# Layer 1's x with tokens on partitions, by 32x32 squares on VectorE and transfers through DRAM in place of TensorE transposes

## The chip, the cores and the metric

The kernel runs on one core of a Trainium2 chip. The core has TensorE (PE, matrix products), VectorE (DVE), ScalarE (ACT), GpSimd (POOL) and SyncE (SP), which issues the transfers, and 16 DMA engines. Each engine runs its own instructions in the order in which they were written into its queue, and waits on semaphores for the others. The metric is the device time of one execution in microseconds (us). Before the change it is 2448.67 us, the median of 3 runs (2447.55 to 2448.9).

## The reference

Four layers work one after the other on x of shape (4, 512, 32, 32), in fp32: 4 batches, 512 channels, 1,024 tokens. Layer 0 is an attention with 8 heads, layer 1 a linear attention, layer 2 an attention with one head and a layer norm ahead of it, layer 3 an attention with 4 heads and a group norm. The change lies in layer 1:

```python
Q = jnp.einsum('bcn,mc->bmn', xf, wq) + bq[None, :, None]
K = jnp.einsum('bcn,mc->bmn', xf, wk) + bk[None, :, None]
V = jnp.einsum('bcn,oc->bon', xf, wv) + bv[None, :, None]
gate = (jnp.max(xf, axis=-1) + jnp.mean(xf, axis=-1))[:, :, None]
V = gate * V
Qf = jax.nn.softplus(Q).transpose(0, 2, 1)
Kf = jax.nn.softplus(K)
KV = jnp.einsum('bmn,bcn->bmc', Kf, V)
norm = 1.0 / jnp.einsum('bnm,bm->bn', Qf, jnp.sum(Kf, axis=-1) + EPS)
wval = jnp.einsum('bnm,bmc,bn->bcn', Qf, KV, norm)
return x + gamma * wval
```

M is 64: queries and keys have 64 features for each of the 1,024 tokens.

## The kernel before

A batch's x lies in SBUF as `[128, 4, 1024]`: 128 channels of a chunk on the partitions, 4 chunks, 1,024 tokens. Every product of two fp32 matrices is two TensorE instructions of up to 512 columns; a transpose is one.

Layer 1 doesn't compute V. The kernel multiplies the keys with x first and with wv after: `keys_times_x` sums K's features times x over the tokens (64 x 512), `transpose_kx` turns that, and `keys_times_values` multiplies it with `wv1`. A product that sums over tokens needs both operands with tokens on the partitions. For x that is `transpose_x(i)`, i = 0 to 3: two blocks of 128 tokens, 4 chunks each, so 8 TensorE transposes into one two-bank PSUM tile (L1438), and a copy of 128x1024 to SBUF, by ScalarE for even i (L1445) and VectorE for odd i (L1443). For the keys it is `transpose_keys` (L1453). The SBUF places for x come from `scratch`, four tiles which `softplus` (e, u, l) and `gates` use as well; xt of i goes to `scratch((i + 3) % 4)`. In batches 0 to 2 they are the tiles `v` of the next batch's layer 0, in batch 3 they are from the pool `pt`.

Layer 1 has no stage of its own. `linear_attention` returns a list of 16 small functions ("pieces"), and the projections of another piece of work call `slot()` after every few products, which takes one piece off the list. For batches 0 to 2 that is `project_qkv` of the next batch in layer 0: one slot after the first 16 products, then a slot after every two calls of `seven_products` (L712), and the last pieces in `project_v` (L837). For batch 3 the pieces stand between products of layer 2's weights (L646) and its first projection. The pieces are, in order: gates, features of both token halves (the second ends with softplus), x's transposes 0, 1, 2, the keys' transposes, x's transposes 3, `keys_times_x` 0 and 1, `keys_times_x` 2 and 3 with `sum_keys`, `divide_queries`, `transpose_kx`, `keys_times_values`, an empty one, and two updates of x.

TensorE keeps the order in which its instructions are written (`manual_schedule`). The other engines' order is set by a planner, which goes by the order of the code as a priority and fills an engine's gaps with what is ready. SP's transfers stand in one queue. DRAM tiles are used already: x of a finished batch is stored to `home` and read back, and the quotients of the attention take a way through `quotients` to be spread over partitions.

softplus (L1390 to L1396) goes back and forth between VectorE and ScalarE and ends with a VectorE instruction that writes `feat`, the queries' and keys' features (`block` in the profile).

Of the kernel before, what the change touches and what calls it, by code (L numbers as in the profile page):

```python
# [13 lines left out]
F32 = mybir.dt.float32  # L14
# [4 lines left out]
P = 128  # L19
# [3 lines left out]
NC = C // P  # L23
NT = S // P
TB = 512
NTB = S // TB
QT = TB // P
M = 64
GROUP = 16
LIMIT = 1e18  # L30


# [18 lines left out]
def general_path(ctx: ExitStack, tc: tile.TileContext, d: dict, out: bass.AP):  # L51
# [41 lines left out]
    for b in range(1, B):  # L93
# [19 lines left out]

    gmat = const.tile([P, P // GROUP, GROUP], F32, name="gmat")
    nc.vector.memset(gmat, 1.0 / GROUP)
    nc.gpsimd.affine_select(
        out=gmat, in_=gmat, pattern=[[-GROUP, P // GROUP], [0, GROUP]],
        compare_op=ALU.is_ge, fill=0.0, base=0, channel_multiplier=1,
    )
    nc.gpsimd.affine_select(  # L120
        out=gmat, in_=gmat, pattern=[[GROUP, P // GROUP], [0, GROUP]],
        compare_op=ALU.is_ge, fill=0.0, base=GROUP - 1, channel_multiplier=-1,
    )
# [351 lines left out]
def plain_path(ctx: ExitStack, tc: tile.TileContext, d: dict, out: bass.AP, count):  # L475
# [11 lines left out]
    nc = tc.nc  # L487
# [7 lines left out]
    dram = ctx.enter_context(tc.tile_pool(name="dram", bufs=1, space=bass.MemoryType.DRAM))  # L495
# [3 lines left out]
    def acc_tile():  # L499
        return ps_acc.tile([P, TB], F32, tag="acc", name="acc")  # L500

    def two_tile(name):
        return ps_sc.tile([P, 2, TB], F32, tag="sc", name=name)

    def row_tile(name):
        return work.tile([P, TB], F32, tag="row", bufs=3, name=name)
# [7 lines left out]
    def many_tile(name):  # L514
        return work.tile([P, NC, TB], F32, tag="many", name=name)
# [9 lines left out]
    def chunks_tile(tag, name, bufs=1):  # L525
        return work.tile([P, NC, TB], F32, tag=tag, bufs=bufs, name=name)
# [69 lines left out]


    wv1 = chunks_tile("xn", "wv1", 2)
    nc.sync.dma_start(wv1, d["wv1"].rearrange("(c p) o -> p c o", p=P))
    block1 = chunks_tile("xn", "block1", 2)  # L600
    wqk1 = block1[:, 0, :].rearrange("p (c o) -> p c o", c=NC)
    nc.sync.dma_start(wqk1, d["wqk1"].rearrange("(c p) o -> p c o", p=P))
# [15 lines left out]
    ident = const.tile([P, P], F32, name="ident")  # L618
# [9 lines left out]

    gmat = const.tile([P, P // GROUP, GROUP], F32, name="gmat")
    nc.vector.memset(gmat, 1.0 / GROUP)  # L630
# [36 lines left out]
    idle = lambda: None  # L667
# [3 lines left out]
    def both(*fs):  # L671
        return lambda: [f() for f in fs]
# [194 lines left out]
    def project_qkv(wqkv, bias, src, vt, room, first=False, between=lambda: None):  # L867

        q = q_tiles()
        k = work.tile([P, NC, S], F32, tag="k", name="k")  # L870
        inputs = lambda j, tb: src(tb)[:, 2 * j : 2 * j + 2, :]
        made = []

        def sums():
            with tc.issue_after(closing.pop()) if closing else nullcontext():
                made.extend(sum_inputs([pt_tile("t") for _ in range(4)], inputs))
            return made


        seven_products(  # L880
            NC,
            lambda i, j, o: wqkv[:, 2 * j : 2 * j + 2, i * C + o * P : i * C + (o + 1) * P],
            inputs,
            lambda i, o: col(bias, i * NC + o),
            lambda i, tb, o: k[:, o, bass.ts(tb, TB)] if i else q[tb][:, o, :],
            sums,
            slots=1,
            first=first,
        )

        assert len(pieces) <= 7
        wv = wqkv[:, :, 2 * C :]
        between()
        project_v(vt, wv, inputs, made, room())
        return q, k
# [502 lines left out]
    def linear_attention(b, scratch):  # L1398

        x = xs[b]  # L1400
        t = {}
        flat = lambda tile: tile.rearrange("p a s -> p (a s)")
# [29 lines left out]
            nc.vector.tensor_scalar(gate, gate, gamma, None, ALU.mult)  # L1432

        def transpose_x(i):
            ps = two_tile("xt")
            for s in range(2):
                for c in range(NC):
                    nc.tensor.transpose(  # L1438
                        ps[:, s, bass.ts(c, P)], x[:, c, bass.ts(2 * i + s, P)], ident
                    )  # L1440
            t["xt", i] = scratch((i + 3) % 4)
            if i % 2:
                nc.vector.tensor_copy(t["xt", i], ps)  # L1443
            else:
                nc.scalar.copy(t["xt", i], ps)  # L1445

        def transpose_keys():

# [16 lines left out]
        def keys_times_x(i):  # L1465
            if i == 0:
                t["kx"] = acc_tile()
            xt = t.pop(("xt", i))

            for s in range(2):  # L1470
                nc.tensor.matmul(  # L1471
                    t["kx"][s * M : (s + 1) * M, :], lhsT=t["kf"][:, 2 * i + s, :],
                    rhs=xt[:, s, :], start=(i == 0), stop=(i == NT // 2 - 1),
                )
            if i == NT // 2 - 1:
                kx = row_tile("kx")
                nc.scalar.copy(kx, t["kx"])
                t["kx"] = kx
# [47 lines left out]
        def update(a):  # L1526
# [15 lines left out]
            lambda: features(0),  # L1542
            lambda: features(1),
            lambda: transpose_x(0),
            lambda: transpose_x(1),
            lambda: transpose_x(2),
            transpose_keys,
            lambda: transpose_x(3),
            both(lambda: keys_times_x(0), lambda: keys_times_x(1)),
            both(lambda: keys_times_x(2), lambda: keys_times_x(3), sum_keys),  # L1550
            divide_queries,
            transpose_kx,
# [102 lines left out]
    def verdict():  # L1655

        assert next(unit) <= UNITS
        ok = const.tile([P, 2 * UNITS], F32, name="ok")
        nc.vector.tensor_scalar(ok, tops.rearrange("p a n -> p (a n)"), LIMIT, None, ALU.is_le)
        row = const.tile([P, 1], F32, name="row")  # L1660
# [6 lines left out]
    with tc.manual_schedule(engines={mybir.EngineType.PE}):  # L1667
# [8 lines left out]
        for b in range(B):  # L1676
            vt = v_tiles()
            if b > 0:
                pieces.extend(linear_attention(b - 1, lambda i: vt[i]))
            q, k = project_qkv(  # L1680
                wqkv0, "bqkv0", lambda tb: xs[b][:, :, bass.ts(tb, TB)], vt,
                lambda: chunks_tile("ot", "ws"), first=(b == 0),
                between=outputs_bias,
            )
            flush()
            if b > 0:
                away(b - 1)
                if b + 1 < B:
                    nc.sync.dma_start(x_tile(b + 1), xin[b + 1])
                else:  # L1690
                    back(0)
            if b == 0:
                os = output_sums(wo0)
            if b == B - 1:
                w2 = wpool.tile([P, 3 * NC, C], F32, tag="wqkv", name="w2")
                nc.sync.dma_start(w2, d["w2"].rearrange("(c p) o -> p c o", p=P))
            attention(
                b, q, lambda c, j: k[:, c, bass.ts(j, P)], vt, 8, 64.0**-0.5, wo0, os, bo0[0],
                plain=(b == B - 1),
            )  # L1700
# [31 lines left out]
        flush()  # L1732
        wo2 = load_wo(d["wo2"])
        lin = linear_attention(B - 1, lambda i: pt_tile("l1"))

        norms[1][0]()
# [4 lines left out]
        for o in range(NC):  # L1741
            ps = gps.get(o)
            if ps is None:
                ps = acc_tile()
# [5 lines left out]
        for o in range(NC):  # L1750
            ps = acc_tile()
# [85 lines left out]
        for b in range(B):  # L1837
            vt = v_tiles()

            q, k = project_qkv(  # L1840
                wqkv3, "bqkv3", lambda tb: ready[tb], vt,
                lambda: wpool.tile([P, NC, C], F32, tag="wo", name="ws") if b == 0
                else chunks_tile("ot", "ws"),
            )
# [20 lines left out]
@with_exitstack  # L1865
def conv_seq(ctx: ExitStack, tc: tile.TileContext, d: dict, out: bass.AP):
    nc = tc.nc
    flag = ctx.enter_context(tc.tile_pool(name="flag", bufs=1))
    count = flag.tile([1, 1], mybir.dt.int32, name="count")
    plain_path(tc, d, out, count)  # L1870
    good = nc.values_load(count, min_val=0, max_val=P)
    with tc.If(good < P):
        general_path(tc, d, out)
# [56 lines left out]
```

## Time and profile before

| what | value |
|---|---|
| median of 3 runs | 2448.67 us |
| the profiled execution | 2449.81 us |
| its span from first to last instruction | 2448.0 us |
| PE busy | 2430.2 us (99%) |
| VectorE busy | 1490.6 us (61%) |
| ScalarE busy | 705.6 us (29%) |
| transposes of x (L1438) | 128, listed at 272 ns each |
| copies of xt by ScalarE (L1445), by VectorE (L1443) | 8 at 1.01 us, 8 at 1.22 us |
| products of keys and x (L1471) | 64, 592 ns each |
| moved by DMA | 87.59 MB, 36 GB/s on average |

Busy time is the union of an engine's instructions. TensorE's instructions overlap, so the distance between two starts, not the listed duration, is what one of them takes from the engine. A line number is that of the instruction in the code below; a group `xt<-ident,x` writes the tile xt and reads ident and x. An entry in square brackets at the end of a timeline row is the engine's idle time before it and who ended it.

### The profile page before, as it was taken

What the parts mean: (1) busy time and instruction counts of PE and PEld (TensorE: products, weight loads), DVE (VectorE), ACT (ScalarE), POOL (GpSimd) and SP (SyncE); (2) the same over time, 40 slices, a digit from 0 to 9 for tenths busy, and PEclk for the clock granted to TensorE, in tenths of its full rate; (3) what the DMA queues carried; (4) which work ended last, traced back from release to release, by engine and by line L of the source; (5) the groups of instructions that cost most, each with busy time, mean ns of one, the idle gap of its engine ahead of it and who ended that gap; (6) DMA issues with size and microseconds to landing.
All of it is one profiled execution on the core that took longest, in us unless ns stands there. A gap on an engine that the chain in (4) does not pass through costs nothing.

```text
span 2448.0 us, 24708 instructions
## 1 busy us (share of the span) xinstructions
PE 2430.2 (99%) x10130; PEld 1220.0 (50%) x10130; DVE 1490.6 (61%) x1778; ACT 705.6 (29%) x868; POOL 248.3 (10%) x240
## 2 busy tenths in 40 slices
PE   9999999999999999999999999999999999999998
PEld 4544544453455344644645446445556456555653
DVE  3577577757765788556595775764554554445344
ACT  1454144415531653221211201112321430321132
POOL 4001100110010002101103021021020001002000
PEclk9999999999999999999999999999999999999999
DMA  5000020002001211011001020110010001000001
GB/s 185 6 13 18 1 78 10 18 1 79 19 9 38 102 27 43 1 69 52 17 0 69 5 85 1 52 69 17 35 69 0 18 35 52 0 35 35 0 27 40
DMA packets 28799, 87.59 MB, mean 36 GB/s; under 512 B 2604, under 2 KB 10284, under 8 KB 25735
## 3 DMA queue, kind: packets, MB, share of 16 engines
q1 hardware_dynamic: 28678, 85.95, 9.7%
q8 instruction: 81, 1.33, 0.2%
q14 instruction: 40, 0.32, 0.0%
HBM read 60.59 MB, written 25.35 MB: 35 GB/s over the span
## 4 chain that ended last, share of the span: by engine, by line
PE 98%; DVE 1%; DMA 0%; ACT 0%; issue 0%; SPq 0%; DVEq 0%
PE acc L712 20%; PE acc L837 12%; PE acc L987 9%; PE sc L941 9%; PE acc L972 9%; PE sc L936 9%; PE acc L844 8%; PE acc L1089 7%; PE acc L1321 6%; PE acc L1282 2%; PE acc L1023 1%; PE acc L646 1%; PE upd L1531 1%; PE acc L1471 1%; PE feat L1413 1%; PE xt L1438 1%
## 5 line engine op out<-in xcount | busy, mean ns | idle before, releaser
L946 ACT ACTIVATE pt<-sc 128x1024 f32<-128x1024 f32 x384 | 379.2, 1022 | 541.2 <-PE sc L941 304.0
L955 DVE TENSOR_TENSOR sum<-sum,pt 128x1024 f32<-128x1024 f32 x256 | 314.5, 1228 | 160.4 <-ACT pt L946 147.4
L972 PE MATMUL acc<-pt,v 64*64 64x512 f32 x2048 | 246.7, 591 | 0.0
L936 PE MATMUL sc<-q,k 64*64 64x512 f32 x2048 | 244.3, 591 | 1.1 <-ACT pt L946 1.1
L987 PE MATMUL acc<-pt,v 128*128 128x512 f32 x512 | 240.8, 594 | 0.0
L941 PE MATMUL sc<-q,k 128*128 128x512 f32 x512 | 239.8, 593 | 0.0
L712 PE MATMUL acc<-t,ws 128*128 128x512 f32 x384 | 173.9, 593 | 0.0
L700 POOL TENSOR_TENSOR ws<-wqkv 128x256 f32<-128x256 f32 (+1 forms) x40 | 37.0, 926 | 1309.9 <-PE acc L1023 519.5
L952 DVE TENSOR_TENSOR sum<-pt 128x1024 f32<-128x1024 f32 x64 | 78.0, 1219 | 137.4 <-ACT pt L946 137.4
L987 PEld LDWEIGHTS acc<-pt,v 128*128 128x128 f32 x512 | 96.6, 190 | 125.3 <-issue 121.6
L941 PEld LDWEIGHTS sc<-q,k 128*128 128x128 f32 x512 | 96.8, 190 | 116.1 <-issue 92.9
L972 PEld LDWEIGHTS acc<-pt,v 64*64 64x64 f32 x2048 | 78.6, 133 | 142.2 <-issue 137.8
L936 PEld LDWEIGHTS sc<-q,k 64*64 64x64 f32 x2048 | 77.4, 133 | 140.8 <-issue 130.7
L712 PEld LDWEIGHTS acc<-t,ws 128*128 128x128 f32 x384 | 72.5, 190 | 86.6 <-issue 85.4
L751 ACT COPY v<-acc 128x512 f32<-128x512 f32 x24 | 14.0, 585 | 306.2 <-PE acc L837 287.9
L683 DVE RECIPROCAL rd<-acc 128x512 f32<-128x512 f32 (+1 forms) x24 | 80.5, 3353 | 29.1 <-PE acc L1023 29.1
L837 PE MATMUL acc<-ws,t 128*128 128x256 f32 x384 | 86.8, 379 | 0.0
L844 PE MATMUL acc<-qs,w 128*128 128x512 f32 x192 | 86.3, 592 | 0.0
L844 PE MATMUL acc<-q,ln 128*128 128x512 f32 x192 | 85.8, 593 | 0.0
L1089 PE MATMUL acc<-ot,wo 128*128 128x256 f32 x336 | 80.6, 383 | 3.2 <-ACT ou L1108 2.7
L742 DVE TENSOR_TENSOR v<-acc,v 128x512 f32<-128x512 f32 x72 | 49.6, 689 | 53.7 <-PE acc L837 53.7
L751 ACT COPY q<-acc 128x512 f32<-128x512 f32 x40 | 23.4, 585 | 197.5 <-PE acc L712 197.5
(328 smaller groups left out, 3450.1 us busy)
## 6 DMA issues: line engine op xcount, KB each, us to landing
home<-x SPq DMA_DIRECT2D x8, 2048.0 KB
x<-home SPq DMA_DIRECT2D x8, 2048.0 KB
out<-x SPq DMA_DIRECT2D x32, 256.0 KB
rds<-quotients SPq DMA_DIRECT2D x30, 256.0 KB
rds<-quotients SPq DMA_DIRECT2D x7, 1024.0 KB
x<-in_x SPq DMA_DIRECT2D x3, 2048.0 KB
wo<-in_wo SPq DMA_DIRECT2D x3, 1024.0 KB
w<-in_w SPq DMA_DIRECT2D x1, 3072.0 KB
```

The source lines that it names most:

```text
L683: nc.vector.reciprocal(rd, ps)
L712: nc.tensor.matmul(ps, lhsT=w[:, m, :], rhs=x[:, m, :], start=start, stop=stop, skip_group_check=True)
L837: nc.tensor.matmul(ps[:, bass.ts(r, C // 2)], lhsT=x[:, m, bass.ts(2 * o + r, P)], rhs=w[:, m, :], start=(start and r == 0), stop=stop, sk ...
L844: nc.tensor.matmul(ps, lhsT=x[:, m, bass.ts(o, P)], rhs=w[:, m, :], start=start, stop=stop, skip_group_check=True,)
L936: nc.tensor.matmul(ps[half(h), s, :], lhsT=key(g, i)[half(s), half(h)], rhs=q[qb][half(s), g, :], start=True, stop=True,)
L941: nc.tensor.matmul(ps[:, s, :], lhsT=key(g, 2 * i + s), rhs=q[qb][:, g, :], start=True, stop=True)
L946: exps.append(nc.scalar.activation(pt, ps, AF.Exp, scale=scale).ins)
L955: adds.append(nc.vector.tensor_tensor(acc, acc, pt, ALU.add).ins)
L972: nc.tensor.matmul(outs[qb, g][r][half(s), :], lhsT=v[i // 2][half(r), i % 2, g * P + s * hd : g * P + (s + 1) * hd], rhs=pt[half(r), s, : ...
L987: nc.tensor.matmul(outs[qb, g][0], lhsT=v[j // 2][:, j % 2, bass.ts(g, P)], rhs=pt[:, s, :], start=(j == 0), stop=(j == NT - 1),)
L1089: nc.tensor.matmul(ps[i][:, bass.ts(o, n)], lhsT=w[:, m, bass.ts(o, P)], rhs=t[:, m, :], start=(start and m + o == 0), stop=(stop and m == ...
L1321: nc.tensor.matmul(ps[i, o], lhsT=w[m][:, bass.ts(o, P)], rhs=t[m], start=(start and m == 0), stop=(stop and m == 3), skip_group_check=True,)
```

## The change

`transpose_x(i)` is written anew and called twice for each batch, each call for 512 tokens. Two VectorE instructions of 128x1024 elements transpose squares of 32x32: within each group of 32 partitions, 32 channels and 32 tokens change places. The result, `squares`, has tokens on the partitions, but only 32 of them, and a quarter of the channels in each group of partitions. Four transfers, one for each group of 32 partitions, store it to a DRAM tile `home` in rows of 2 KB (1 MB in all). Two transfers of 512 KB read it back in rows of 1 KB, with 128 tokens on the partitions, into the same four `scratch` places as before. `squares` is the tile of the tag `many`, of which there is one; of `home` there are two.

The channels of xt then stand in another order: group of 32, chunk, channel within the 32. `keys_times_x` picks one token block's columns out of xt as runs of 32 elements with a step of 64, and `wv1` is loaded with its rows in that order, by four transfers of 32 partitions in place of one.

In the list of pieces, x's transposes are pieces 4 and 5; the places of the former third and fourth are empty. The keys' transposes stand in the same, seventh place, between the two empty ones.

```diff
-    nc.sync.dma_start(wv1, d["wv1"].rearrange("(c p) o -> p c o", p=P))
+
+    rows = d["wv1"].rearrange("(c a j) o -> c j a o", c=NC, a=NC)
+    for c in range(NC):
+        nc.sync.dma_start(wv1[c * SQUARE : (c + 1) * SQUARE], rows[c])
...
         def transpose_x(i):
-            ps = two_tile("xt")
-            for s in range(2):
-                for c in range(NC):
-                    nc.tensor.transpose(
-                        ps[:, s, bass.ts(c, P)], x[:, c, bass.ts(2 * i + s, P)], ident
-                    )
-            t["xt", i] = scratch((i + 3) % 4)
-            if i % 2:
-                nc.vector.tensor_copy(t["xt", i], ps)
-            else:
-                nc.scalar.copy(t["xt", i], ps)
...
+            squares = many_tile("squares").rearrange(
+                "p r (h n j) -> p r h n j", h=2, n=2 * NC
+            )
+            for h in range(2):
+                k = 2 * i + h
+                nc.vector.transpose(
+                    squares[:, :, h].rearrange("p r n j -> p n r j"),
+                    x[:, :, k * 2 * P : (k + 1) * 2 * P].rearrange(
+                        "p c (n j) -> p c n j", j=SQUARE
+                    ),
+                )
+            home = dram.tile([NC, NC, SQUARE, TB], F32, tag="squares", bufs=2, name="squares")
+            for a in range(NC):
+                nc.sync.dma_start(
+                    home[a].rearrange("r i f -> i r f"),
+                    squares[a * SQUARE : (a + 1) * SQUARE].rearrange("p r h n j -> p r (h n j)"),
+                )
+            for h in range(2):
+                xt = t["xt", 2 * i + h] = scratch((2 * i + h + 3) % 4)
+                nc.sync.dma_start(
+                    flat(xt).rearrange("p (a f) -> p a f", a=NC),
+                    home.rearrange("a r i (h f) -> h (r i) a f", h=2)[h],
+                )
...
-            xt = t.pop(("xt", i))
+            xt = flat(t.pop(("xt", i))).rearrange("p (b s j) -> p s b j", s=2, j=SQUARE)
...
-                    rhs=xt[:, s, :], start=(i == 0), stop=(i == NT // 2 - 1),
+                    rhs=xt[:, s], start=(i == 0), stop=(i == NT // 2 - 1),
...
             lambda: transpose_x(0),
             lambda: transpose_x(1),
-            lambda: transpose_x(2),
+            idle,
             transpose_keys,
-            lambda: transpose_x(3),
+            idle,
```

More of the change, by code (lines that the diff above doesn't have):

```diff
@@ L29 @@
 GROUP = 16
+SQUARE = 32
 LIMIT = 1e18
```

## The prediction

> **What bounds the kernel now.** I read the page first: busy time by engine, then the chain that ended last.
>
> ```profile
> PE 2430.2 (99%) x10130; PEld 1220.0 (50%) x10130; DVE 1490.6 (61%) x1778; ACT 705.6 (29%) x868; POOL 248.3 (10%) x240
> ...
> PE 98%; DVE 1%; DMA 0%; ACT 0%; issue 0%; SPq 0%; DVEq 0%
> ```
>
> TensorE is the bound from end to end, so a removed TensorE instruction shortens the span unless a wait takes its place. Next, the waits of PE (total, times, longest):
>
> ```profile
> PE acc L712 <- DMA wqkv<-in_wqkv: 4.9, 1, 4.9
> PE acc L1089 <- ACT ou L1108: 2.7, 4, 0.7
> PE sc L936 <- ACT pt L946: 1.1, 4, 0.3
> ```
>
> The largest is the first load; none lies in a layer 1 stage. Then PE's timeline of batch 0's layer 1 (start, duration of the merged row):
>
> ```profile
> 250.19 1.88 PE L712 MATMUL acc<-t,ws 128*128 128x512 f32 x4
> 251.90 1.04 PE L1438 MATMUL xt<-ident,x 128*128 128x128 f32 x8
> 252.78 1.88 PE L712 MATMUL acc<-x,ws 128*128 128x512 f32 x4
> ...
> 260.52 1.04 PE L1438 MATMUL xt<-ident,x 128*128 128x128 f32 x8
> 261.40 3.60 PE L712 MATMUL acc<-t,ws 128*128 128x512 f32 x8
> 264.93 0.47 PE L1453 MATMUL keys<-ident,block 64*128 64x64 f32 x8
> ```
>
> A transpose is listed at 272 ns, but they are pipelined: eight hold PE from 251.90 to 252.78, 0.88 us. And VectorE's timeline, batch 0, then batch 3:
>
> ```profile
> 244.89 0.75 DVE L744 SCALAR_TENSOR_TENSOR k<-acc,cols,k 128x512 f32<-128x512 f32 x1 [1.03 <-PE acc L712]
> 249.78 1.22 DVE L1390 SCALAR_TENSOR_TENSOR v<-block 128x1024 f32<-128x1024 f32 x1 [4.14 <-ACT block L1418]
> ...
> 259.64 1.21 DVE L1443 COPY v<-xt 128x1024 f32<-128x1024 f32 x1
> 260.77 0.73 DVE L744 SCALAR_TENSOR_TENSOR k<-acc,cols,q 128x512 f32<-128x512 f32 x1
> 261.43 1.21 DVE L1396 SCALAR_TENSOR_TENSOR block<-block,v 128x1024 f32<-128x1024 f32 x1
> ```
>
> ```profile
> 947.91 4.41 DVE L1427 TENSOR_REDUCE gate<-x 128x4 f32<-128x4096 f32 x1
> ...
> 970.23 3.35 DVE L1593 RECIPROCAL rstd<-rstd 128x512 f32<-128x512 f32 x1 [3.54 <-ACT rstd L1592]
> ...
> 994.44 1.22 DVE L1396 SCALAR_TENSOR_TENSOR block<-block,l 128x1024 f32<-128x1024 f32 x1
> ```
>
> Three things to see. L1396, softplus's last step, ends at 262.64 and the keys' transposes (L1453) start at 264.93: 2.3 us of room. In batch 3 L1396 ends at 995.66 and L1453 starts at 996.42: 0.8 us. And VectorE has holes before softplus: 4.14 us and 3.54 us. L1427 shows that its order is not PE's: its piece stands in the slot that PE reaches near 958, yet it ran at 947.91, as soon as x was final.
>
> [...] no transpose is in this trace, and the 128x1024 passes take 1.21 to 1.23 us. [...]
>
> ```profile
> 118.05 0.62 SPq L1035 DMA_DIRECT2D quotients<-rd  x1
> 119.81 1.31 SPq L1038 DMA_DIRECT2D rds<-quotients  x2
> ...
> 312.67 0.34 SPq L573 DMA_DIRECT2D home<-x  x1
> 319.94 0.39 SPq L1689 DMA_DIRECT2D x<-in_x  x1
> ```
>
> 8 KB to DRAM hold the next issue for 1.76 us, 2 MB for 7.27 us.
>
> **Part by part.**
>
> Removed on PE: 16 groups of eight transposes, 0.87 to 0.88 us each, 3.51 us a batch: 14.0 us, all on the bounding engine. Removed on ACT: 8 copies (L1445, 1.01 us); on VectorE: 8 copies (L1443, 1.22 us). Their two-bank PSUM tiles go too; nobody waits for one, worth nothing.
>
> Added on VectorE: 16 transposes of 128x1024. [...] I take 1.2 us. They read x alone, so the holes before softplus can take the first two, as L1427 went ahead.
>
> Added on SP: 12 issues a batch, 0.4 to 0.8 us each (the trace has 0.43 for 128 rows of 2 KB, 0.80 for 512 rows). A write of 1 MB: 1.76 + (7.27 - 1.76) / 2 = 4.5 us. A read of 512 KB in 1 KB rows: 0.8 issue, 1.3 us at the 390 GB/s that the loads from 14 to 24 us reached or twice that, 1.2 completion: 3.3 to 4.7; I take 4.0, its twin 1.3 later. VectorE's second call must wait for the first writes, as "squares" has one buffer. Chain from the first transpose: 2.4 + 4.5 + 5.3 = 12.2 us to the second xt; 2.4 + 4.5 + 2.4 + 4.5 + 5.3 = 19.1 us to the fourth. The products with keys stand at 273.27 and 278.77, 3.5 us earlier without the transposes: 269.8 and 275.3. Even if VectorE begins only at the old place, 251.9, they are due after 17.9 and 23.4 us: hidden with 4 to 6 us to spare; beginning in the hole at 245.6 gives about 6 us more. On SP, the read into scratch(0) must wait for softplus's e (free after L1394, 257.9 before) and the second call's writes queue behind it: then 258 + 4.5 + 5.3 = 268, still in time. SP has nothing else queued until 312.67 (batch 3: 1044.33). Traffic grows by 16.8 MB, in stages where the page shows little.
>
> The key transposes keep the seventh place in the list (the diff puts idle pieces around them; a slot later than before it does not put them). But three of the removed groups stood ahead: PE comes to them 2.6 us earlier, at 262.3. What is late next is softplus. Batches 0 to 2: 262.6 less 1.1 (VectorE copy inside it) less 1.0 (ACT's copy between its exponential and its logarithm) plus two transposes of the second call, half of their 2.4 us in the holes where VectorE waits for ACT: 261.7, so no wait; I charge 0.3 each. If all four fall into softplus uncovered: 265.3, a wait of 3.0. Batch 3: PE comes at 993.8; L1396 ends at 995.7 - 1.1 = 994.5 with no transpose inside, 999.3 with four: a wait of 0.7 to 5.5; I take 1.5. A transpose ahead of a join of the products holds a PSUM buffer up to 1.2 us; four buffers cover most: 0.6 in all.
>
> wv1 in four issues instead of one, at 14 us: its first use is at 292.9, cost nothing; uncovered it would be three issues, 1.3 us. The strided operand of 64 products: from nothing to 64 x 0.43 = 27 us if it halves their rate; I take nothing.
>
> Sum: -14.0 + 0.9 + 1.5 + 0.6 = -11.0 us on a span of 2448.0, so 2437.0. The profiled execution took 2449.81, 1.8 outside the span and 1.1 above the median of 2448.67; from that median: 2437.7 us.
>
> **Rivals.**
>
> 1. Keys' wait takes the gain. If VectorE's order puts all transposes at their own slots, inside softplus, PE stands 3.0 us in each of three batches and 5.5 in the fourth: 14.5 of 14.0 returned, about 2449. For it: 0.8 us of room in batch 3. Against: L1427 and the two holes. Partly so, 2441 to 2444.
>
> 2. Slower: the round trip becomes the wait at the products with keys (L1471). The chain is 19.1 us against 23.4 from the old place; it costs from 23.4 on, has eaten the gain at 23.4 + 3.5 = 26.9, and decides for slower at 28.1 (4.9 us over four batches more). With write and read twice as slow (9.0 and 10.6) from the old place: 2.4 + 9.0 + 2.4 + 9.0 + 10.6 = 33.4, 10 us late, four times, minus 14: 2475. For it: 2 KB and 1 KB rows from 32 partitions at a time, which no row here measures. Against: 390 GB/s at 2 KB rows.
>
> 3. VectorE itself stands still behind the second call's transposes for the writes (4.5 us), with the products' joins queued behind them and PE behind those: about 2 to 3 us a batch, 2446 to 2449.
>
> That the transposes leave PE is certain from the code; that the new path gives PE less to do is not a rival.
>
> **How the numbers follow.** Forecast 0.75 (own range 2434.5 to 2443.5, the lower end with no wait at all); rival 1 in full 0.11; rival 2 with the strided operand 0.08; rival 3 0.06. About 0.2%, 4.9 us, is what a measurement can tell from no change: faster 0.75, same 0.14 (rival 1, half of rival 3), slower 0.11. The range of 2434 to 2448.5 leaves out rival 2 and the far half of 1 and 3.
>
> **What would show it.** Right: L1438 gone, PE busy near 2416; VectorE transposes of about 1.2 us, the first before L1390; no PE wait on DMA at L1471; a small wait of L1453 on L1396, largest in batch 3. Wrong: PE waiting for xt's transfers, transposes above 2 us, L1471 above 0.43 us apart, or joins late behind a VectorE that waits for a DMA.

## The result, and the profile after

The kernel after takes 2436.03 us (median of 5 runs, 2434.6 to 2436.72), the kernel before, beside it on the same chip, 2448.62 us (5 runs, 2447.55 to 2448.9). The ratio is 0.9949, with a 95% interval of 0.9938 to 0.9960: 12.6 us faster, where 11.0 were forecast. Up to the end of `gates` a line's number is that of before plus 4 (L712 is L716, softplus's L1390 to L1396 are L1394 to L1400). The keys' transposes are L1475, the products with keys L1493, the new VectorE transposes L1450, the writes to DRAM L1458 and the reads L1464.

The page of after, busy time by engine and the chain that ended last:

```profile
PE 2416.0 (99%) x10002; PEld 1203.5 (49%) x10002; DVE 1497.2 (62%) x1786; ACT 697.6 (29%) x860; POOL 250.8 (10%) x240
...
PE 98%; DVE 1%; ACT 1%; issue 0%; DMA 0%; SPq 0%; DVEq 0%
```

TensorE has 128 instructions and 14.2 us less to do (2430.2 before) and is still the bound. The span went from 2448.0 to 2433.0 us.

The waits of PE after (total, times, longest):

```profile
PE acc L716 <- DMA wqkv<-in_wqkv: 4.3, 1, 4.3
...
PE acc L716 <- DVE q L789: 1.2, 1, 1.2
...
PE acc L1008 <- DVE ot L987: 0.6, 1, 0.6
```

Neither the keys' transposes (L1475) nor the products with keys (L1493) are in it: no wait on softplus there, and none on the round trip through DRAM. Two waits are new, L789 and L987, once each, both around batch 3's layer 1.

PE's timeline of batch 0's layer 1 after (start, duration of the merged row):

```profile
248.54 1.88 PE L716 MATMUL acc<-t,ws 128*128 128x512 f32 x4
250.25 1.88 PE L716 MATMUL acc<-x,ws 128*128 128x512 f32 x4
...
260.65 0.47 PE L1475 MATMUL keys<-ident,block 64*128 64x64 f32 x8
...
268.11 1.94 PE L1493 MATMUL acc<-v,kf 128*64 128x512 f32 x8
269.98 1.98 PE L716 MATMUL acc<-x,ws 128*128 128x512 f32 x4
```

Where the transposes stood, products of the projection follow one another: the next row starts at 250.25, 1.71 us after 248.54, as its like did before (250.19 to 251.90). The eight products with the strided operand hold PE from 268.11 to 269.98, 1.87 us; before, the same row took 1.86 us:

```profile
273.27 1.94 PE L1471 MATMUL acc<-v,kf 128*64 128x512 f32 x8
275.13 1.98 PE L712 MATMUL acc<-x,ws 128*128 128x512 f32 x4
```

Over these eight products the strides cost 0.01 us.

VectorE's timeline around the same batch:

```profile
212.69 1.24 DVE L1450 STREAM_TRANSPOSE squares<-x 128x1024 f32<-128x1024 f32 x1
...
248.13 1.23 DVE L1394 SCALAR_TENSOR_TENSOR v<-block 128x1024 f32<-128x1024 f32 x1 [4.14 <-ACT block L1422]
...
257.04 1.21 DVE L1400 SCALAR_TENSOR_TENSOR block<-block,v 128x1024 f32<-128x1024 f32 x1
```

The other three of the batch start at 217.23, 232.66 and 241.07, so all four are over before softplus begins. The first call needs tokens 0 to 511 alone, and these are final when layer 0 has finished their half; so the first transpose ran at 212.69, some 37 us ahead of the slot in which its piece stands (250.25) and 23 us before the gates' pass over the whole of x (L1431, at 236.07). softplus ends at 258.25 and PE comes to the keys at 260.65: 2.4 us of room.

SP's timeline (duration is that of the issue; x4 and x3 are the issues of one call):

```profile
218.49 2.88 SPq L1458 DMA_DIRECT2D squares<-squares  x4
240.79 0.38 SPq L1464 DMA_DIRECT2D v<-squares  x1
...
254.12 4.51 SPq L1464 DMA_DIRECT2D v<-squares  x3
```

The first write left at 218.49, the second call's at 242.34; the first read waited until 240.79 for a scratch place that the gates held (16.1 us, behind L1434 on ScalarE), not for the data. The other three reads left from 254.12 on, as softplus gave its places back. They are due at 268.11 and 273.61.

**Where the 12.6 us came from.** I compared the start of the same PE instruction in both traces, stage by stage (after less before):

| stretch | difference gained or lost, us |
|---|---|
| first 22 us (first load, and what follows it) | -1.65 |
| layer 1 of batch 0 | -3.50 |
| attention of batch 1 | -0.54 |
| layer 1 of batch 1 | -3.46 |
| layer 1 of batch 2 | -3.52 |
| end of batch 3's attention in layer 0 | +1.40 |
| layer 1 of batch 3 | -1.94 |
| last stores | -1.6 |

The first row is not the change's: a lead of 0.65 to 1.9 us at 22 us is in every other run below, in that of a kernel whose time doesn't differ from before too (wv1 alone, the last experiment). The last row is not explained. From the issue of the last store to the end it is 6.3 us in the trace of before, 6.1 with wv1 alone, and 4.6 to 5.1 in the changed kernel and in every variant of it below; no run tries what makes this, and I leave it out of the sum. The other six sum to -11.56 us. A second profile of the changed kernel, ahead by 0.65 us at the start and by 12.21 in batch 3, gives the same: 12.21 - 0.65 = 11.56.

So three batches pay in full, 3.5 us each, and batch 3 pays 0.54 net. The first loss of batch 3 lies before its layer 1. VectorE and then PE at the end of layer 0's last attention, after:

```profile
893.91 1.23 DVE L1450 STREAM_TRANSPOSE squares<-x 128x1024 f32<-128x1024 f32 x1
...
899.84 0.68 DVE L987 TENSOR_TENSOR ot<-ot,acc 128x512 f32<-128x512 f32 x1
```

```profile
898.09 1.04 PE L976 MATMUL acc<-pt,v 64*64 64x512 f32 x8
...
900.58 0.65 PE L1008 MATMUL acc<-sum,ones 64*64 64x512 f32 x3 [0.61 <-DVE ot L987]
```

L987 adds the upper half of an output out of PSUM and so gives a PSUM place back. Before, as L983, it started 0.35 us after the last row of output products, VectorE and then PE:

```profile
911.11 0.68 DVE L983 TENSOR_TENSOR ot<-ot,acc 128x512 f32<-128x512 f32 x1
```

```profile
910.76 1.04 PE L972 MATMUL acc<-pt,v 64*64 64x512 f32 x8
911.62 1.30 PE L1004 MATMUL acc<-sum,ones 64*64 64x512 f32 x8
```

After, it starts 1.75 us behind that row (899.84 and 898.09). Two transposes of 1.2 us, the one shown and one at 891.65, stand a little ahead of it, VectorE has no gap between them and it, and PE waits.

The second loss is inside batch 3's layer 1, VectorE and then PE:

```profile
978.57 1.22 DVE L1398 SCALAR_TENSOR_TENSOR l<-l,l 128x1024 f32<-128x1024 f32 x1 [1.66 <-ACT l L1397]
979.71 0.68 DVE L789 TENSOR_TENSOR q<-q,acc 128x512 f32<-128x512 f32 x1
```

```profile
972.18 7.11 PE L716 MATMUL acc<-w,ws 128*128 128x512 f32 x16
980.45 1.98 PE L716 MATMUL acc<-w,gq 128*128 128x512 f32 x4 [1.16 <-DVE q L789]
```

Before, PE had transposes of x between and behind the same products:

```profile
984.27 3.60 PE L712 MATMUL acc<-w,ws 128*128 128x512 f32 x8
987.70 1.04 PE L1438 MATMUL xt<-ident,x 128*128 128x128 f32 x8
988.58 3.60 PE L712 MATMUL acc<-w,ws 128*128 128x512 f32 x8
992.01 1.04 PE L1438 MATMUL xt<-ident,x 128*128 128x128 f32 x8
```

A join (L789), which frees a PSUM place, is queued behind softplus's L1398, which waits 1.66 us for ScalarE's logarithm. No transpose is near. PE comes earlier than before and finds softplus no further than ScalarE lets it be; softplus ends at 983.26, and the keys' transposes follow at 984.08 without a wait. From start to start the 16 products take 8.27 us (972.18 to 980.45), where they took twice 3.43 before: 1.41 lost. The row behind the wait takes 0.10 longer than before (980.45 to 982.27, against 992.89 to 994.61) and a row ahead of it 0.06 (968.59 to 972.18, against 979.86 to 983.39). The three sum to 1.57, all that batch 3's layer 1 lacks of 3.51.

### The profile page after: what moved, and what is told of

The parts are those of the page before. It is cut to its first block, busy times and chain, and to the rows that moved or that the text cites. A ratio compares the mean times of both kernels' runs of the same rounds, so it can differ in the third digit from the quotient of the medians.

```text
span 2433.0 us, 24544 instructions
## 1 busy us (share of the span) xinstructions
PE 2416.0 (99%) x10002; PEld 1203.5 (49%) x10002; DVE 1497.2 (62%) x1786; ACT 697.6 (29%) x860; POOL 250.8 (10%) x240
## 4 chain that ended last, share of the span: by engine, by line
PE 98%; DVE 1%; ACT 1%; issue 0%; DMA 0%; SPq 0%; DVEq 0%
PE acc L716 19%; PE acc L841 12%; PE acc L976 9%; PE acc L991 9%; PE sc L945 9%; PE sc L940 9%; PE acc L848 8%; PE acc L1093 7%; PE acc L1325 6%; PE acc L1286 2%; PE acc L1027 1%; PE acc L650 1%; PE upd L1553 1%; PE acc L1493 1%; PE kv L650 1%; PE feat L650 1%
## 5 line engine op out<-in xcount | busy, mean ns | idle before, releaser
L716 PE MATMUL acc<-t,ws 128*128 128x512 f32 x384 | 173.9, 593 | 0.0
L716 PEld LDWEIGHTS acc<-t,ws 128*128 128x128 f32 x384 | 72.7, 190 | 88.0 <-issue 87.3
```

The source lines that it names most:

```text
L716: nc.tensor.matmul(ps, lhsT=w[:, m, :], rhs=x[:, m, :], start=start, stop=stop, skip_group_check=True)
```

## The experiments

My theory: the gain is PE's time, one for one, and the round trip and the transposes cost nothing in batches 0 to 2 because they run early, in VectorE's and SP's idle time; batch 3 loses to what PE now waits for. The rivals: the new path costs something everywhere, so that a kernel without it would be faster by several us; the early start doesn't matter, since the trip would be hidden from its old place too; and the keys' wait.

The kernels of the first four experiments ran together, beside before at 2447.82 us (9 runs, 2447.09 to 2448.51); the last four, on another chip, beside before at 2447.57 us (31 runs, 2446.93 to 2449.1). Where one of the last four is compared with the changed kernel, that kernel's time is the one from the first chip.

### The changed kernel again

> The changed kernel once more, so that the next three have it beside them on the same chip. Theory (cover): PE gets 14.0 us back, 3.5 in each batch; batches 0 to 2 keep all of it, batch 3's layer 1 keeps 1.9, and 1.4 are lost at the end of layer 0's attention of batch 3. So 2436.0, within 1.5, and the same steps in the trace: -3.5, -3.5, -3.5, +1.4, -1.9. The other 1.65 us by which the trace of the first profile was ahead at 22 us, and 1.6 at its end, are of those two executions and not of the change: in a new pair they come out otherwise.

Measured: 2436.04 us (2435.59 to 2436.62), ratio 0.9952 (0.9939 to 0.9966). It is the mark for what follows.

### The products without the new path

```diff
-            xt = flat(t.pop(("xt", i))).rearrange("p (b s j) -> p s b j", s=2, j=SQUARE)
+            xt = x[:, i, :].rearrange("p (s f) -> p s f", s=2)
...
-            lambda: transpose_x(0),
-            lambda: transpose_x(1),
+            idle,
+            idle,
```

> The products of keys and x take x itself as their right-hand operand: no transposes, no transfers, only the 64 products as before, so layer 1's values are not computed; all other work stays. Theory (cover): the new path costs nothing in batches 0 to 2; in batch 3 the 1.4 us at the end of the attention come back, and the join that waits behind softplus (1.2 us) stays, as no transpose stands there: 2434.6 (2433.0 to 2435.5). Rival (the round trip, or VectorE's added work, costs a little in every batch): 2431 or less.

Measured: 2434.09 us (2433.78 to 2434.65), ratio 0.9945 (0.9931 to 0.9959). All of the new path together, transposes, writes and reads, costs 1.95 us, and the trace says where: in batches 0 to 2 it gains no more than the changed kernel (its difference after batch 2 is -11.77, that of the changed kernel profiled again -11.66); what it lacks is the loss at the end of batch 3's attention (it gains another 0.2 us there, where the changed kernel loses 1.4). In PE's waits of this kernel no line names L987, and this one is left:

```profile
PE acc L716 <- DVE q L789: 1.2, 1, 1.2
```

So the new path made the wait on L987. The wait on L789 stays, with no transposes and no transfers in the kernel: it is softplus, overtaken by a PE with less to do.

### Batch 3 as before

```diff
+        pe = b == B - 1
...
-            lambda: transpose_x(0),
-            lambda: transpose_x(1),
-            idle,
-            transpose_keys,
-            idle,
+            *([lambda: transpose_x_pe(0), lambda: transpose_x_pe(1), lambda: transpose_x_pe(2),
+               transpose_keys, lambda: transpose_x_pe(3)] if pe else
+              [lambda: transpose_x(0), lambda: transpose_x(1), idle, transpose_keys, idle]),
```

`transpose_x_pe` is the old `transpose_x`; in batch 3 kx is copied into the order of the new `wv1`.

> Batches 0 to 2 as changed, batch 3 with TensorE's transposes and copies as before (the sums of keys times x are put in wv1's order by the copy out of PSUM). Theory (cover, batch 3 lost most): PE gets 3.5 us more to do, 1.4 at the end of the attention and some 1.6 behind softplus come back: +0.5, 2436.5 (2435.0 to 2437.5). Rival (every batch gains alike): +3.5 to the changed kernel, 2439.5.

Measured: 2436.12 us (2435.5 to 2436.63), ratio 0.9952 (0.9939 to 0.9966): the time of the changed kernel within 0.1 us. Its difference to before stays within 0.3 us from the end of batch 2 (-12.13) to the last product, and neither L789 nor L987 is among PE's waits. Three batches earn the whole gain; in batch 3 the change gives back what it takes.

### Batch 3's transposes held behind the add

```diff
+    uppers = []
...
-                    nc.vector.tensor_tensor(o, o, upper, ALU.add)
+                    uppers[:] = [nc.vector.tensor_tensor(o, o, upper, ALU.add).ins]
...
-                nc.vector.transpose(
-                    squares[:, :, h].rearrange("p r n j -> p n r j"),
+                with tc.issue_after(uppers[-1]) if b == B - 1 else nullcontext():
+                    nc.vector.transpose(
+                        squares[:, :, h].rearrange("p r n j -> p n r j"),
```

> The changed kernel with batch 3's transposes queued on VectorE behind the last addition that frees PSUM in layer 0's attention. Theory (VectorE's order in batch 3): the wait of the row sums' matrix products on that addition goes, -1.4, and everything else stays: 2434.6, with no jump at the end of the attention in the trace. Rival (the loss there has another cause, or comes back in softplus because the transposes are now late): no change, 2436.0 or more.

Measured: 2433.79 us (2432.99 to 2434.11), ratio 0.9943 (0.9929 to 0.9957). It beats both kernels: 14.0 us less than before and 2.25 less than the changed kernel on the same chip, whose fastest run (2435.59) is slower than its slowest. It is as fast as the kernel without the path (2434.09), so the path now costs nothing that these runs show. VectorE, then PE, at the end of batch 3's attention (this kernel's lines are one number up on after's):

```profile
898.19 0.68 DVE L988 TENSOR_TENSOR ot<-ot,acc 128x512 f32<-128x512 f32 x1
...
914.23 2.36 DVE L1452 STREAM_TRANSPOSE squares<-x 128x1024 f32<-128x1024 f32 x2
```

```profile
897.97 1.04 PE L977 MATMUL acc<-pt,v 64*64 64x512 f32 x8
898.83 1.18 PE L1009 MATMUL acc<-sum,ones 64*64 64x512 f32 x8
```

The add starts 0.22 us after the row of output products, not 1.75, and PE's eight products with ones follow in one row, with no wait. The edit names the last such add of the attention, at 913.63, so the first call's two transposes run behind that one, some 22 us later than in the changed kernel and still 39 us ahead of the second call's. Between the two traces 1.5 us of the difference lie at this place; the rest lies in the first 22 us and in the last stores. The wait of 1.2 us on the join in batch 3's layer 1 is still there.

### All transposes after softplus

```diff
-        nc.vector.scalar_tensor_tensor(z, z, 0.0, l, ALU.max, ALU.add)
+        return nc.vector.scalar_tensor_tensor(z, z, 0.0, l, ALU.max, ALU.add).ins
...
-            softplus(feat, *(flat(scratch(i)) for i in range(3)))
+            t["last"] = softplus(feat, *(flat(scratch(i)) for i in range(3)))
...
-                nc.vector.transpose(
+                with tc.issue_after(t["last"]):
+                    nc.vector.transpose(
```

> The changed kernel with all transposes of 32x32 queued on VectorE behind softplus's last step. Theory (the early start is the cover): in batch 0 they then begin at 258.3 instead of 212.7. First call 258.3 to 261, stored by 265.8, read back by 269.5 against products due at 268.1: 1.4 us late; second call 265.8 to 268.5, stored by 273, read by 276.5 against about 275: 1.5 more. 3 us in each batch, 12 in all: 2448 (2443 to 2454), with PE waiting for transfers at the products of keys and x, and none on the keys' transposes. Rival (the round trip has room wherever the transposes stand): 2436.

Measured: 2473.49 us (2470.14 to 2475.05), ratio 1.0107 (1.009 to 1.0124): slower than before by 26 us and than the changed kernel by 37, three times what I had expected. The place is the one named. PE's waits (lines are again one number up on after's):

```profile
PE acc L1494 <- DMA v<-squares: 15.7, 8, 3.5
PE acc L1494 <- DMA l<-squares: 7.5, 3, 5.4
```

These are 23.2 of the 37 us. The stages lose more than the waits say (8.0, 8.0, 9.3 and 11.6 us to the changed kernel), and the trace shows where the rest goes: to the clock that TensorE was granted. In batch 0 it is 1.00 ahead of the first wait (262 to 268), 0.50 behind it (271.39 to 275.00), and 1.00 again from 278 on. The two rows behind that wait take 6.56 us from start to start (271.39 to 277.95, the rows below), where the changed kernel's take 3.69 (268.11 to 271.80). These 2.9 us and the waits of 3.44, 1.01 and 0.35 are 7.7 of the 8.0. The whole trace has six such stretches, 30.7 us at 0.50, each beginning in or just behind a wait for a read, and its mean granted clock is 0.993; the trace of the changed kernel has none in its layer 1 stages, and a mean of 1.000.

VectorE's first transpose of batch 0, and SP's writes and reads:

```profile
258.59 1.23 DVE L1451 STREAM_TRANSPOSE squares<-x 128x1024 f32<-128x1024 f32 x1
```

```profile
261.57 2.88 SPq L1459 DMA_DIRECT2D squares<-squares  x4
267.86 0.94 SPq L1465 DMA_DIRECT2D v<-squares  x2
270.98 2.86 SPq L1459 DMA_DIRECT2D squares<-squares  x4
277.10 0.93 SPq L1465 DMA_DIRECT2D v<-squares  x2
```

Here nothing but the data holds the reads, so the steps of the trip can be read: a write takes 6.3 us from its first issue to the issue of the read that waits for it (261.57 to 267.86), the second call's 6.1 (from 270.98 to 277.10). PE's products wait for the reads:

```profile
271.39 3.68 PE L1494 MATMUL acc<-v,kf 128*64 128x512 f32 x8 [3.44 <-DMA v<-squares]
275.00 3.11 PE L716 MATMUL acc<-x,ws 128*128 128x512 f32 x4
277.95 1.88 PE L716 MATMUL acc<-t,ws 128*128 128x512 f32 x4
280.84 1.08 PE L1494 MATMUL acc<-v,kf 128*64 128x512 f32 x4 [1.01 <-DMA v<-squares]
282.27 1.08 PE L1494 MATMUL acc<-v,kf 128*64 128x512 f32 x4 [0.35 <-DMA v<-squares]
```

A read is there 3.5 us after its issue (267.86 to 271.39), 3.7 for the first of the second call and 5.2 for its twin (277.10 to 280.84 and 282.27). From the first transpose to the fourth xt it is 258.59 to 282.27: 23.7 us. So a start this late is paid for in every batch, 8.0 to 11.6 us, once as a wait and once more at the clock of 0.50. It is later than the old place would be: that slot stands at 250.02 in this trace, 8.6 us before 258.59. No run has the transposes there.

### The keys one slot earlier

```diff
-            idle,
             transpose_keys,
             idle,
+            idle,
```

> The changed kernel with the keys' transposes one piece earlier, ahead of the first empty piece instead of behind it. Theory: PE comes to them at 256.7 in batch 0, softplus ends at 258.3: 1.5 us of wait in batches 0 to 2; in batch 3 the end of softplus is 2.8 behind PE: 7.3 in all, 2443 (2440 to 2445). Rival (the place of the keys' transposes does not matter, other work fills the time): 2436.

Measured: 2443.66 us (2442.46 to 2445.43), ratio 0.9983 (0.9977 to 0.999), as expected. PE's waits:

```profile
PE keys L1475 <- DVE block L1400: 7.4, 4, 4.0
```

7.4 us of wait answer to the 7.6 us by which it is slower than the changed kernel. The keys' wait is real, and one slot away; the empty piece that the diff puts ahead of the keys is worth these 7.6 us, more than half of the gain. The longest of the four waits, 4.0 us, is batch 3's, and behind it the clock is 0.50 for 3.4 us; behind the other three, 1.1 us each, it stays at 1.00.

### A longer trip

```diff
+            again = dram.tile([NC, NC, SQUARE, TB], F32, tag="again", bufs=2, name="again")
+            nc.sync.dma_start(
+                again.rearrange("a r i f -> (a r i) f"), home.rearrange("a r i f -> (a r i) f")
+            )
...
-                    home.rearrange("a r i (h f) -> h (r i) a f", h=2)[h],
+                    again.rearrange("a r i (h f) -> h (r i) a f", h=2)[h],
```

> The changed kernel with one more transfer in the trip: after the store, 1 MB from DRAM to DRAM, and the read back from there; some 5 us more for each call. Theory (cover): the reads wait for softplus to free their places anyway, and their data is due about 10 us after they land: no change, 2436.0 within 1. Rival (the trip is at its limit): each us of it counts four times, +10 to +20, 2446 to 2456.

Measured: 2435.91 us (2435.01 to 2436.68), ratio 0.9952 (0.9935 to 0.9968): no change. SP's timeline in batch 0, the second call's copy and the reads behind it:

```profile
255.57 0.49 SPq L1463 DMA_DIRECT2D again<-squares  x1
261.83 0.93 SPq L1468 DMA_DIRECT2D v<-again  x2
```

The write takes 6.26 us here as well (219.39 to 225.65, the first call), the copy another 6.26 (255.57 to 261.83), and the products don't wait. With the start as early as in the changed kernel the trip has more than 6 us of slack at the call that is later.

### wv1 in four loads, alone

The kernel before, with its `wv1` loaded as the diff does and kx copied into that order; the transposes stay on PE.

```diff
-    nc.sync.dma_start(wv1, d["wv1"].rearrange("(c p) o -> p c o", p=P))
+    rows = d["wv1"].rearrange("(c a j) o -> c j a o", c=NC, a=NC)
+    for c in range(NC):
+        nc.sync.dma_start(wv1[c * 32 : (c + 1) * 32], rows[c])
```

> The kernel before with wv1 loaded in four transfers in the new order of rows, and the copy of the sums of keys times x out of PSUM in the same order; nothing else is changed. Theory: no difference, 2448.6 within 1. Rival (the 1.65 us by which the changed kernel was ahead at 22 us come from this load): 2447.0, and its trace ahead by as much at 22 us.

Measured: 2447.66 us (2447.12 to 2448.8), ratio 1.0001 (0.9992 to 1.001). The loads cost nothing. Its trace is ahead of that of before by 1.35 us at 22 us, at the same time of the whole: this is why I don't count the first row of the table above. In batch 1's attention it gains another 0.23, with no change to layer 1.

## Why the prediction was right, and where its terms were not

- **PE's part, -14.0 us.** Right: PE's busy time fell by 14.2 us, and batches 0 to 2 gained 3.50, 3.46 and 3.52 us, against 3.51 worked out from the eight transposes that hold PE 0.88 us.
- **VectorE's transposes at 1.2 us.** Right: 1.23 to 1.25 us each. That one in fp32 would take as long as a plain pass of 128x1024, 1.21 to 1.23 us, was my estimate; the trace of before has no such transpose.
- **The strided operand and wv1 at nothing.** Right: 1.87 us against 1.86 for eight products, and a ratio of 1.0001. That runs of 128 bytes would cost nothing was my estimate; the trace of before has no such operand in these products.
- **The keys' wait in batches 0 to 2, 0.9 us.** Wrong: there is none. The step that failed is the one that put the first transposes into the hole before softplus, because "they read x alone" and I took x as final only when the gates' pass over all of it ran. Each call reads half of the tokens, and half of x is final a whole stretch earlier. So no transpose fell inside softplus, and 2.4 us of room were left.
- **The keys' wait in batch 3, 1.5 us.** The layer 1 of batch 3 gained 1.94 instead of 3.51, so 1.57 us went, near to the sum's term; but the wait is at a join of the projection (L789) queued inside softplus, 1.16 us, and not at the keys, and no transpose has a part in it: it stays when the transposes are gone. softplus and ScalarE's functions set the pace there (VectorE waits 1.12 and 1.66 us for them). That the size came near is luck, since the mechanism was another.
- **Joins and PSUM, 0.6 us.** Mis-sized: 1.40 us at one place, the end of batch 3's attention. I had looked for joins of the projection late behind a transpose; it was an add of the attention before, since transposes that are ready early also stand in the way early. Holding them behind that attention's last add gains 2.25 us.
- **The round trip, hidden "with 4 to 6 us to spare" even from the old place.** Right that it is hidden, wrong in this margin. The chain to the fourth xt is 23.7 us instead of 19.1. The term mis-sized is the write, 4.5 us taken and 6.3 and 6.1 measured: 3.4 of the 4.6 us. Another 1.3 are joins that VectorE does between the transposes or ahead of them (3.0 us from the first transpose to the first write, 3.1 from the first reads to the second write, not 2.4 each), which the sum had at nothing. The reads were right: 5.2 us with the twin, 5.3 taken, 1.2 of it for a completion (in the trace of before the reads of `quotients` wait 1.17 us for their write, the mean of 23). By this chain, an estimate, transposes begun at 251.9 would have brought the fourth xt at 275.6, with the products due at 275.3: nothing to spare, but not much to pay either, and no run tries it. Shown is that the start some 37 us ahead of the slot leaves room (the longer trip) and that a start behind softplus leaves none. The price for the write was a line through two transfers of other shapes, 8 KB and rows of 16 KB, and it should have carried its upper end through to the result.
- **The rivals.** The keys' wait (the first) and the round trip as the wait (the second) are both real mechanisms of this kernel, shown with the keys one slot earlier (+7.6 us) and with late transposes (+37 us). The change as it is stays clear of both. For the third, a VectorE that stands still behind the second call, the trace has nothing: 15 us lie between the first call's last transpose (217.23) and the second call's first (232.66), filled with other work, and a write takes 6.3.

The forecast of -11.0 us against -11.56 by the traces and -12.6 by the times is nearer than its terms were, and that is in part luck: 0.9 too much for the keys and 0.54 not foreseen in batch 1's attention lie on one side, 0.8 too little for the joins on the other. What made batch 1's attention gain 0.54 us was not tried; a wait of 0.46 us on L1056's output, which the trace of before shows there, is absent in all changed kernels. With wv1 alone that wait is 0.2 and the stretch 0.23 us shorter, so part of the 0.54 may come without the change.

## What to carry to other kernels

When one engine bounds, an instruction taken off it counts in full only where the next thing in its line is ready: ask of every stage what that is (here batches 0 to 2 gained 3.5 us each, and batch 3's layer 1, where softplus was not ready, 1.94). Whether work moved to an engine with idle time is hidden depends on when it starts as well as on how long it is: here a trip 6 us longer cost nothing, and a start 46 us later cost 37 us. So find for each part the earliest moment at which its own inputs are final, half a tile if it reads half. And work that becomes ready early can be put ahead of a small instruction that frees a buffer: an order edge there was worth 2.25 us. A wait of the bounding engine can cost more than its length: here the waits for the late reads were 23.2 of the 37 us, and in or behind them the granted clock was 0.50 for 30.7 us in all.

## What the runs showed of the hardware

- A write of 1 MB to DRAM as four transfers of 32 partitions each, in 2 KB rows, takes 6.1 to 6.3 us from first issue to the issue of the read that waits for it, in seven of the eight calls of the kernel with late transposes (6.9 in the eighth); in the trace of before 2 MB in rows of 16 KB held the next issue for 6.25 to 6.37 us at five places and for 7.27 us at a sixth (312.67). Half the bytes took about as long here.
- A copy of 1 MB from DRAM to DRAM takes 6.26 us; a read of 512 KB in 1 KB rows 3.5 to 3.7 us, its twin 1.4 us later.
- The 32x32 transpose of 128x1024 fp32 elements takes 1.23 to 1.25 us (16 in the trace of after), with reads and writes that step over squares, about as long as the 1.21 to 1.23 us of plain passes of that size.
- With late transposes the clock granted to TensorE was 0.50 for 3.4 or 6.8 us, six times in one trace: five times behind a wait of 2.8 to 5.4 us for a read, once behind two waits of 1.7 and 0.4 us in a row. With the keys one slot earlier it was 0.50 for 3.4 us behind the wait of 4.0 us. Behind single waits of 1.0 to 1.2 us it stayed at 1.00.
